# Holding weight loads behind the projections' weights, and splitting the experts' weights, in a Mamba-2 + MLP + mixture-of-experts kernel

## The chip, the cores and the metric

The kernel runs on one core of a Trainium2 chip. Time is device time in microseconds (us), from launch to the end of the program. A core has TensorE (PE in the profile; its weight load is PEld), VectorE (DVE), ScalarE (ACT), GpSimd (POOL) and SyncE (SP). Each works through its own instructions in the order in which the program lists them, and waits at an instruction until the semaphores it needs are there. DMAs are issued by SyncE (most loads), ScalarE (stores) and GpSimd (gathers and scatters by index); 16 DMA engines carry them.

## The reference

Input x has 2048 rows of 512 floats. All is float32.

```
a = layernorm(x)
r = rmsnorm(a, ln1);  z, xb, B, C, dt = split(r @ in_proj)      # 512 -> 2576
xb, B, C = silu(causal conv over 4 rows)
y = chunked state space recurrence (16 heads, chunks of 128 rows) + D * xb
h = a + rmsnorm(y * silu(z), norm_w) @ out_proj                 # 1024 -> 512
m = h + (silu(h2 @ gate) * (h2 @ up)) @ down,  h2 = rmsnorm(h, ln2)   # 512 -> 2048 -> 512
x1 = x + m
n = layernorm(x1);  the two best of 8 experts for each row, weights by softmax
out = x1 + sum over the two of weight * ((silu(n @ Wg[e]) * (n @ Wu[e])) @ Wd[e])   # 512 -> 352 -> 512
```

## The kernel before

The rows are worked in 8 blocks of 256 (two chunks of 128 each) for the recurrence, in 4 blocks of 512 for the MLP, and in tiles of 128 rows sorted by expert for the experts.

**Normalisation and projection.** `load_x` brings x in by 128 rows (t = 0 to 15), into five buffers; the first four are loaded at the start, the fifth (t = 4, the first of block 2; the program calls it x_524) when block 0's recurrence begins in the program. `prepare(b)` takes the statistics of the block's two row tiles (L149, L150), normalises them to `hn` (L219), turns them (L201) into `hT` (L205), and makes from `hT` the time steps `pdt` (L239) and, through a chain of small operations on VectorE and Exp on ScalarE, the decays. These go through DRAM (`rowsd`, L278, L279) and come back spread over the partitions as `cum` and `ec` (`spread`, L312, L324). `first_rows` holds block 1's statistics behind those of block 0; block 2's are not held. The projection of a block takes ten pairs of 128 columns: six (`project`: xb, B, C) and four (`gate`: z). Each pair's weight `wi` (512 KB) is loaded two pairs ahead into three buffers (`load_w_in`, L99), so a load waits until TensorE is done with the pair three before. `project` copies the product out of PSUM on ScalarE (`pre`, L352), VectorE makes the convolution (`ca`, L359, L361), ScalarE the silu (L367). Block 0's six pairs come first, alone; from then on each block's recurrence runs beside the next block's projection.

**Recurrence.** `chunk` takes Exp of `cum` on ScalarE (L420), multiplies on VectorE (L422), the products on TensorE (L414, L437, L445, L452), and the output projection with `w_o` (2048 KB, loaded once, L803; scaled once on POOL, L813; used at L490).

**MLP.** `feed_forward(fb)` works 16 pieces of 128 of the 2048 hidden columns. Its products are made by a scheme that saves multiplications and needs sums of the weights: for fb = 0 `load_early` and `load_late` load the raw parts (`mg`: three loads of 128 KB, `ms`: one of 256 KB) and POOL makes the sums (L531, L532, L542, L543), which ScalarE stores to DRAM; later fb load the stored sums. `mg` and `ms` share three buffers. `load_down` loads the second matrix, 256 KB each piece (`md`, four buffers, L552). fb = 0 begins on TensorE in block 2, at about 222 us.

**Experts.** During the last MLP block `load_expert` loads all eight experts (`ew`, 1408 KB of Wg and Wu and 704 KB of Wd each): a one-column copy on POOL that reads the newest MLP product paces each load.

**What sets the order.** A scheduler orders each engine's instructions (TensorE's from block 2 on is fixed by the program), with its own idea of how long a load takes; `tc.issue_after(i)` makes what is inside wait its turn behind the instruction `i` in the order of issue. SyncE's loads are one queue.

Of the kernel before, what the change touches and what calls it, by code (L numbers as in the profile page):

```python
# [16 lines left out]
P = 128  # L17
T = 2048
D = 512
NK = D // P  # L20
# [14 lines left out]
NE = 8  # L35
EI = 352
# [18 lines left out]
def mamba_mlp_moe(ctx, tc, x, w_in, w_out, w_gu, w_down, par, wr, wg, wu, wd, out):  # L55
# [3 lines left out]
    nc = tc.nc  # L59
# [27 lines left out]
    w_o = pw.tile([P, 8, D], F32, name="w_o")  # L87
# [5 lines left out]
    w_in_k = w_in.rearrange("(k p) n -> p k n", p=P)  # L93
    nc.sync.dma_start(out=w_dt, in_=w_in_k[:, :, 2560:2576])

    def load_w_in(pair):

        w = pw.tile([P, NK, 2 * P], F32, name="wi", tag="wi", bufs=3)
        nc.sync.dma_start(out=w, in_=w_in_k[:, :, pair * 2 * P : (pair + 1) * 2 * P])  # L99
        return w  # L100

    ahead = [load_w_in(pair) for pair in range(2)]
# [9 lines left out]
        out=tri, in_=ones, pattern=[[1, P]], compare_op=ALU.is_ge, fill=0.0, base=0, channel_multiplier=-1  # L112
# [192 lines left out]
    def spread(b, j, rows_d):  # L305

        t = b * NCH + j
        heads = rows_d[:, j * NH : (j + 1) * NH, :]
        cum = []
        for gp in range(2):  # L310
            c = wa.tile([P, 8, P], F32, name=f"cum{t}_{gp}", tag="cum", bufs=3)
            nc.sync.dma_start(out=c, in_=bc(heads[0, 8 * gp : 8 * gp + 8], 0, P))  # L312

            nc.gpsimd.affine_select(  # L314
                out=c, in_=c, pattern=[[0, 8], [1, P]], compare_op=ALU.is_ge, fill=-3.0e38,
                base=0, channel_multiplier=-1,
            )
            cum.append(c)
        ec = None
        if t:  # L320
            ec = wa.tile([P, 2, 4, P], F32, name=f"ec{t}", tag="ec")
            for g in range(4):
                part = slice(g % 2 * HD, (g % 2 + 1) * HD)
                nc.sync.dma_start(out=ec[part, g // 2], in_=bc(heads[1, 4 * g : 4 * g + 4], 0, HD))  # L324
        return cum, ec

    def finish(steps):
        while True:
            try:
                next(steps)  # L330
            except StopIteration as end:
                return end.value
# [187 lines left out]
    KH = NK // 2  # L520
# [3 lines left out]
    def load_early(fb, c):  # L524

        w = pmlp.tile([P, 4, KH, FC], F32, name="mg", tag="mg", bufs=3)
        if fb == 0:
            nc.sync.dma_start(out=w[:, 0], in_=w_gu[c, :, 0, 0])
            nc.sync.dma_start(out=w[:, 1], in_=w_gu[c, :, 1, 1])
            nc.sync.dma_start(out=w[:, 3], in_=w_gu[c, :, 1, 0])  # L530
            nc.gpsimd.tensor_tensor(w[:, 1], w[:, 3], w[:, 1], ALU.add)  # L531
            nc.gpsimd.tensor_tensor(w[:, 2], w[:, 1], w[:, 0], ALU.subtract)  # L532
        else:
            nc.sync.dma_start(out=w[:, 0:3], in_=early_d[c])
        return w
# [14 lines left out]
    def load_down(c):  # L550
        d = pmlp.tile([P, D], F32, name="md", tag="md", bufs=4)
        nc.sync.dma_start(out=d, in_=w_down[c * FC : (c + 1) * FC, :])  # L552
        return d
# [12 lines left out]
    newest = None  # L566
# [127 lines left out]
    def feed_forward(fb):  # L694

        nonlocal mlp_w, newest
        if fb == 0:
            w = load_early(0, 0)
            mlp_w = w, load_late(0, 0, w)
        b11, b21, b22, t1, t2, t3, t4 = sums(fb)  # L700
        rows = []
        pair = None
        made = {}

        def product(ps, w, m, first=True):
            for k in range(KH):
                nc.tensor.matmul(  # L707
                    ps, w[:, k], m[:, k], start=(first and k == 0), stop=(k == KH - 1), skip_group_check=True
                )

        early, late = mlp_w
        for c in range(NFC):
            more = fb < NFB - 1 or c < NFC - 1
            to = (fb, c + 1) if c < NFC - 1 else (fb + 1, 0)
            if more:
                coming = load_early(*to)
            if c == 1:  # L720
                for j in range(NJ):
                    rows.append(wk.tile([P, D], F32, name=f"r{fb}_{j}", tag="row", bufs=5))
                    nc.sync.dma_start(out=rows[j], in_=resd[fb * NJ + j])
            if c > 1 and c % 2 == 0:
                pair = [made.pop(n) for n in (c - 2, c - 1)]
            a = wk.tile([P, 2, FH], F32, name=f"a{fb}_{c}", tag="a", bufs=4)
            up = wk.tile([P, FH], F32, name=f"up{fb}_{c}", tag="up", bufs=2)
            x1 = bank("g", [FH], f"px{fb}_{c}")
            x2 = bank("u", [FH], f"py{fb}_{c}")

            def p2():
                product(x2, late[:, 2], b21)
                with tc.high_priority(AT_ONCE):
                    nc.vector.tensor_tensor(a[:, 0], a[:, 0], x2, ALU.add)
                nc.scalar.activation(a[:, 0], a[:, 0], AF.Silu)

            def p3():
                product(x2, late[:, 1], b22, False)
                with tc.high_priority(AT_ONCE):
                    nc.vector.tensor_tensor(a[:, 1], a[:, 1], x2, ALU.add)  # L740
                nc.scalar.activation(a[:, 1], a[:, 1], AF.Silu)

            def p5():
                product(x2, early[:, 1], t1)
                with tc.high_priority(AT_ONCE):
                    nc.scalar.copy(up, x2)


            order = [p2, p5, p3] if c == 0 else [p5, p3, p2]
            product(x1, early[:, 0], b11)  # L750
            with tc.high_priority(AT_ONCE):
                nc.scalar.copy(a[:, 0], x1)  # L752
            order[0]()
            if pair:
                mlp_down(fb, rows, 2 * (c % 2), pair)
            yield
            product(x1, early[:, 2], t2, False)
            with tc.high_priority(AT_ONCE):
                nc.scalar.copy(a[:, 1], x1)
            order[1]()  # L760
            if more:
                coming = coming, load_late(*to, coming)
            yield
            product(x1, late[:, 0], t3, False)
            with tc.high_priority(AT_ONCE):
                nc.vector.tensor_tensor(up, up, x1, ALU.add)  # L766
            order[2]()
            yield
            product(x1, late[:, 3], t4, False)
            with tc.high_priority(AT_ONCE):  # L770
                nc.vector.tensor_tensor(a[:, 0], a[:, 0], x1, ALU.mult)
            nc.gpsimd.tensor_tensor(a[:, 1], a[:, 1], up, ALU.mult)  # L772
            if pair:
                mlp_down(fb, rows, 2 * (c % 2) + 1, pair)
            newest = a.rearrange("p h q -> p (h q)")
            made[c] = newest, load_down(c)
            if more:
                early, late = coming
            yield
        if more:  # L780
            mlp_w = coming
        pair = [made.pop(n) for n in (NFC - 2, NFC - 1)]
        for j in range(NJ):
            mlp_down(fb, rows, j, pair)
        yield
        yield from route(fb, rows)
# [9 lines left out]
    for pair in range(6):  # L796
        finish(project(0, pair, hT, *xc))
        if pair < 2:
            next(coming)
        elif pair == 2:  # L800
            ready = finish(coming)
            near = [spread(0, 0, ready[-1])]
    nc.sync.dma_start(out=w_o, in_=w_out.rearrange("(t p) n -> p t n", p=P))  # L803
    near.append(spread(0, 1, ready[-1]))
    xbts[0] = turned_x(0, xc[0])

# [109 lines left out]

    def load_expert(e, part):

        gu = ew[:, e, :NG].rearrange("p (k a n) -> p k a n", k=NK, a=2)
        d = ew[:, e, NG:].rearrange("p (m n) -> p m n", m=len(ET))  # L920
        for lo in (part * EI,) if part < 2 else (NG, NG + 2 * D):
            nc.gpsimd.tensor_copy(ew[: EI - 2 * P, e, lo : lo + 1], newest[: EI - 2 * P, 0:1])
        if part < 2:
            nc.sync.dma_start(out=gu[:, :, part, :], in_=(wg, wu)[part][e].rearrange("(k p) n -> p k n", p=P))
        else:
            nc.sync.dma_start(out=d[:, 0:2, :], in_=wd[e, 0 : 2 * P, :].rearrange("(k p) n -> p k n", p=P))
            nc.sync.dma_start(out=d[: EI - 2 * P, 2, :], in_=wd[e, 2 * P : EI, :])


# [75 lines left out]
        first = yield from table(NS1, "1")  # L1005

    tail = routed(tail)
    parts = [(e, part) for e in range(NE) for part in range(3)]
    for n in range(4 * NFC):
        next(feed)  # L1010
        if n % 4 == 2:
            next(tail, None)

        if n % 5 in (0, 2) and parts:
            load_expert(*parts.pop(0))
    assert first and not parts

# [176 lines left out]
```

## Time and profile before

| | us |
|---|---|
| median of 3 runs (lowest to highest) | 1541.81 (1540.99 to 1544.17) |
| the profiled execution's own time | 1540.27 |
| its span, first to last instruction | 1538.6 |
| TensorE matmul busy | 1498.3 |
| VectorE, ScalarE, GpSimd busy | 749.8, 744.0, 425.5 |

The span is shorter than the execution by what lies around the program. A row of the timeline is start, duration, engine, line, operation, tiles (written<-read), shape and count, and in brackets how long the engine had been idle and what ended that. A wait is put down to what came last. The granted clock of TensorE was 0.994 in the mean.

### The profile page before, as it was taken

How to read it: one execution, taken by the hardware profiler on the slowest of the kernel's cores; microseconds unless marked ns; L12 is line 12 of the kernel's file. 1: busy time of each engine (PE TensorE's matmuls, PEld its weight loads, DVE VectorE, ACT ScalarE, POOL GpSimd, SP SyncE). 2: the span in 40 equal slices, each digit the busy share in tenths (PEclk: the TensorE clock that was granted, in tenths of full speed). 3: DMA queues.
4: the chain of work that ended last, by engine and by line, in shares of the span. 5: the costliest groups of instructions: out<-in, count | busy, mean ns of one | idle time of the engine just before them, and what ended most of it. 6: DMA issues, size and time to landing. Idle time of an engine off the chain costs nothing. (4 is left out here: it accounts for less than half of the span.)

```text
span 1538.6 us, 18825 instructions
## 1 busy us (share of the span) xinstructions
PE 1498.3 (97%) x6153; PEld 1021.0 (66%) x6153; DVE 749.8 (49%) x1939; ACT 744.0 (48%) x1332; POOL 425.5 (28%) x537
## 2 busy tenths in 40 slices
PE   8899999999999999999999999999999999999996
PEld 7566577677667676767676677666776666566553
DVE  7776775645645564556454643334343433222221
ACT  5888967635663598458745754222221231111110
POOL 4432324424242212141212120411131124233321
PEclk9999999999999999999999999999999999999999
DMA  9444445545544554454335532426879434333332
GB/s 305 137 138 125 137 140 183 190 149 171 171 151 148 185 165 131 137 118 157 121 123 179 167 121 89 93 93 209 289 205 260 152 91 64 66 69 65 66 63 35
DMA packets 128241, 217.54 MB, mean 141 GB/s; under 512 B 12560, under 2 KB 72848, under 8 KB 128144
## 3 DMA queue, kind: packets, MB, share of 16 engines
q1 hardware_dynamic: 105376, 166.34, 35.6%
q0 software_dynamic: 9088, 18.91, 7.2%
q10 hardware_dynamic: 13680, 31.07, 5.4%
q8 instruction: 52, 0.85, 0.2%
q14 instruction: 45, 0.37, 0.1%
HBM read 175.48 MB, written 40.80 MB: 141 GB/s over the span
## 5 line engine op out<-in xcount | busy, mean ns | idle before, releaser
L691 PE MATMUL pd<-md,a 128*128 128x512 f32 x512 | 238.8, 593 | 0.8 <-DVE r L692 0.7
L340 PE MATMUL pm<-hT,wi 128*128 128x256 f32 x768 | 185.4, 386 | 3.7 <-DMA wi<-in_w_in 3.7
L340 PEld LDWEIGHTS pm<-hT,wi 128*128 128x128 f32 x768 | 141.7, 192 | 29.2 <-issue 7.9
L692 DVE TENSOR_TENSOR r<-r,pd 128x512 f32<-128x512 f32 x128 | 87.4, 684 | 150.6 <-PE pd L691 149.9
L691 PEld LDWEIGHTS pd<-md,a 128*128 128x128 f32 x512 | 96.9, 190 | 76.6 <-issue 65.8
L361 DVE SCALAR_TENSOR_TENSOR ca<-pre,params,ca 128x256 f32<-128x256 f32 x288 | 143.9, 557 | 0.3
L707 PE MATMUL py<-h2T,ms 128*128 128x256 f32 x512 | 131.7, 380 | 3.5 <-DMA ms<-late 2.6
L772 POOL TENSOR_TENSOR a<-a,up 128x256 f32<-128x256 f32 x64 | 47.0, 734 | 265.7 <-DVE up L766 225.8
L340 PE MATMUL pz<-hT,wi 128*128 128x256 f32 x512 | 117.0, 381 | 0.0
L490 PE MATMUL po<-w_o,zs 128*128 128x512 f32 x256 | 116.2, 607 | 0.0
L1045 PE MATMUL epg<-ew,xgT 128*128 x288 | 109.0, 460 | 0.2 <-ACT xgT L203 0.2
L1045 PE MATMUL epu<-ew,xgT 128*128 x288 | 108.7, 459 | 0.0
L707 PEld LDWEIGHTS py<-h2T,ms 128*128 128x128 f32 x512 | 95.4, 190 | 19.5 <-issue 2.3
L420 ACT ACT_TABLE_LOAD x75 | 96.2, 1283 | 21.5 <-DVE ncum L285 14.5
L340 PEld LDWEIGHTS pz<-hT,wi 128*128 128x128 f32 x512 | 94.8, 190 | 13.8 <-ACT zs L373 0.8
L1066 PE MATMUL epd<-ew,ehT 128*128 (+1 forms) x216 | 98.9, 593 | 1.0 <-DVE ehT L1059 1.0
L420 ACT ACTIVATE cum<-cum,ncum 128x128 f32<-128x128 f32 x256 | 85.7, 392 | 6.2 <-POOL cum L314 4.8
L490 PEld LDWEIGHTS po<-w_o,zs 128*128 128x128 f32 x256 | 49.5, 195 | 58.4 <-issue 57.3
L752 ACT COPY a<-px 128x256 f32<-128x256 f32 x64 | 23.6, 369 | 127.2 <-PE px L707 111.3
L1026 POOL DMA_INDIRECT xg<-xnd,idx x36 | 35.5, 985 | 154.4 <-PE pt L201 150.6
L422 DVE SCALAR_TENSOR_TENSOR cum<-cum,dt,psc 128x128 f32<-128x128 f32 x256 | 72.9, 339 | 5.8 <-PE psc L414 3.6
L203 ACT COPY xgT<-pt 128x512 f32<-128x512 f32 x36 | 21.0, 586 | 111.8 <-PE pt L201 111.8
(240 smaller groups left out, 2528.1 us busy)
## 6 DMA issues: line engine op xcount, KB each, us to landing
wi<-in_w_in SPq DMA_DIRECT2D x80, 512.0 KB, 3.8
ms<-late SPq DMA_DIRECT2D x48, 512.0 KB, 3.7
mg<-early SPq DMA_DIRECT2D x48, 384.0 KB, 3.8
md<-in_w_down SPq DMA_DIRECT2D x64, 256.0 KB, 4.0
cum<-rowsd SPq DMA_DIRECT2D x32, 512.0 KB, 4.1
late<-ms ACTq DMA_DIRECT2D x16, 512.0 KB, 2.7
ec<-rowsd SPq DMA_DIRECT2D x60, 128.0 KB, 3.4
xnd<-xn ACTq DMA_DIRECT2D x28, 256.0 KB, 3.8
```

The source lines that it names most:

```text
L340: nc.tensor.matmul(pm[:, m, :], w[:, k, m * P : (m + 1) * P], hT[:, k, :], start=(k == 0), stop=(k == NK - 1))
L361: nc.vector.scalar_tensor_tensor(ca, pre[:, m, k : k + TB], cw[:, k : k + 1], ca, ALU.mult, ALU.add)
L420: nc.scalar.activation(lt[:, half, i], lt[:, half, i], AF.Exp, bias=ncum[:, j, h : h + 1])
L422: nc.vector.scalar_tensor_tensor(lt[:, half, i], lt[:, half, i], dt[:, j, h : h + 1], psc[:, half, i], ALU.mult, ALU.mult)
L490: nc.tensor.matmul(po, y[:, m, :], w_o[:, m, :], start=(m == 0), stop=(m == 7))
L691: nc.tensor.matmul(pd, a[:, j * P : (j + 1) * P], d, start=(m == 0), stop=(m == 1))
L692: nc.vector.tensor_tensor(rows[j], rows[j], pd, ALU.add)
L707: nc.tensor.matmul(ps, w[:, k], m[:, k], start=(first and k == 0), stop=(k == KH - 1), skip_group_check=True)
L772: nc.gpsimd.tensor_tensor(a[:, 1], a[:, 1], up, ALU.mult)
L1026: nc.gpsimd.indirect_dma_start(out=xg, out_offset=None, in_=src, in_offset=bass.IndirectOffsetOnAxis(ap=idx[:, n : n + 1], axis=0))
L1045: nc.tensor.matmul(ps, xT[:, k, :], w[:, lo : lo + EI], start=(k == 0), stop=(k == NK - 1))
L1066: nc.tensor.matmul(pd, hT[:n, m, :], w[:n, NG + m * D : NG + (m + 1) * D], start=(m == 0), stop=(m == len(ET) - 1))
```

## The change

It does three things. `loaded` keeps the newest in-projection weight load; w_o's load, the first MLP's first weights and the first MLP's down weights are placed behind it in the order of issue (w_o behind the load that is newest at the end of block 0's projections, and the first MLP's weights behind the one that is newest when that MLP begins). The first `spread` stands after the fifth projection pair in place of the third. The experts' weights are loaded in 48 pieces (Wg and Wu in halves of 352 KB, Wd in 512 and 192 KB), one on three of four steps of the last MLP block, in place of 24 calls with 32 loads on two of five.

```diff
+    loaded = None
     def load_w_in(pair):
+        nonlocal loaded
         w = pw.tile([P, NK, 2 * P], F32, name="wi", tag="wi", bufs=3)
-        nc.sync.dma_start(out=w, in_=w_in_k[:, :, pair * 2 * P : (pair + 1) * 2 * P])
+        loaded = nc.sync.dma_start(out=w, in_=w_in_k[:, :, pair * 2 * P : (pair + 1) * 2 * P]).ins
...
         if fb == 0:
-            w = load_early(0, 0)
+            with tc.issue_after(loaded):
+                w = load_early(0, 0)
             mlp_w = w, load_late(0, 0, w)
...
-            made[c] = newest, load_down(c)
+            with ExitStack() if fb else tc.issue_after(loaded):
+                made[c] = newest, load_down(c)
...
         elif pair == 2:
             ready = finish(coming)
+        if pair == 4:
             near = [spread(0, 0, ready[-1])]
-    nc.sync.dma_start(out=w_o, in_=w_out.rearrange("(t p) n -> p t n", p=P))
+    with tc.issue_after(loaded):
+        loaded = nc.sync.dma_start(out=w_o, in_=w_out.rearrange("(t p) n -> p t n", p=P)).ins
...
     def load_expert(e, part):
...
-        for lo in (part * EI,) if part < 2 else (NG, NG + 2 * D):
-            nc.gpsimd.tensor_copy(ew[: EI - 2 * P, e, lo : lo + 1], newest[: EI - 2 * P, 0:1])
-        if part < 2:
-            nc.sync.dma_start(out=gu[:, :, part, :], in_=(wg, wu)[part][e].rearrange("(k p) n -> p k n", p=P))
-        else:
-            nc.sync.dma_start(out=d[:, 0:2, :], in_=wd[e, 0 : 2 * P, :].rearrange("(k p) n -> p k n", p=P))
+        half, a = divmod(part, 2)
+        ks = slice(half * KH, (half + 1) * KH)
+        lo = (half * NK + a) * EI if part < 4 else NG + 2 * a * D
+        nc.gpsimd.tensor_copy(ew[: EI - 2 * P, e, lo : lo + 1], newest[: EI - 2 * P, 0:1])
+        if part < 4:
+            nc.sync.dma_start(out=gu[:, ks, a, :], in_=(wg, wu)[a][e].rearrange("(k p) n -> p k n", p=P)[:, ks])
+        elif a == 0:
+            nc.sync.dma_start(out=d[:, 0:2, :], in_=wd[e, 0 : 2 * P, :].rearrange("(k p) n -> p k n", p=P))
+        else:
             nc.sync.dma_start(out=d[: EI - 2 * P, 2, :], in_=wd[e, 2 * P : EI, :])
...
-    parts = [(e, part) for e in range(NE) for part in range(3)]
+    parts = [(e, part) for e in range(NE) for part in range(6)]
...
-        if n % 5 in (0, 2) and parts:
+        if n % 4 != 1 and parts:
```

The scheduler lays the engines' orders anew. SyncE's first loads in both programs (lines of before):

```
before: x x x x params w_dt wi wi wr wi w_o x_524 mg mg wi mg ms mg wi rowsd mg mg md cum
        rowsd cum wi wi cum wi ec*4 wi md md wi md wi cum ...
after:  x x x x params w_dt wi wi wr wi x_524 wi wi rowsd wi rowsd cum wi cum cum wi w_o
        ec*4 wi wi wi cum ...   (mg mg mg ms mg mg mg wi md ms only behind the 32nd wi)
```

VectorE's first instructions, with the statistics of x_524 marked:

```
before: ... stats(x_83) stats(x_85) ... hT hT ... hn v hn u dt ... dA stats(x_524) rows ... ncum ca
after:  ... stats(x_83) stats(x_85) ... stats(x_524) hT hT ... hn v hn u dt ... dA rows ... ncum ca
```

## The prediction

> **What bounds the kernel now.** I read the engine shares first, then who waited for whom, then the first 75 us in order of time, since the page shows that nothing later has room.
>
> ```profile
> PE 1498.3 (97%) x6153; PEld 1021.0 (66%) x6153; DVE 749.8 (49%) x1939; ACT 744.0 (48%) x1332; POOL 425.5 (28%) x537
> ...
> PE pc L273 <- DVE dA L270: 5.3, 3, 2.9
> PE pm L340 <- DMA wi<-in_w_in: 3.7, 1, 3.7
> ...
> PE py L707 <- DMA ms<-late: 2.6, 2, 1.9
> ```
>
> TensorE sets the time: 1498.3 of 1538.6 us. About 40 us are idle, and the change can only save what of these is a DMA's: 3.7 us once for an in-projection weight, and 2.6 us twice in all for an MLP weight. Where the 3.7 us lie, and what comes with them, the timeline (start, duration, engine, line) and the table by stretch (length; busy time of each engine; granted clock, DMA share, GB/s) tell:
>
> ```profile
> 8.31 1.27 DVE L205 TENSOR_TENSOR hT<-pt,params 128x512 f32<-128x512 f32 x2
> ...
> 19.48 0.70 DVE L149 BATCH_NORM_STATS2 bn<-x 128x6 f32<-128x512 f32 x1 [0.37 <-DMA x<-in_x]
> ...
> 9.04 1.96 PE L239 MATMUL pdt<-w_dt,hT 128*128 128x16 f32 x16 [0.75 <-DVE hT L205]
> ...
> 34.08 5.38 PE L340 MATMUL pm<-hT,wi 128*128 128x256 f32 x16 [3.71 <-DMA wi<-in_w_in]
> ...
> 22.89 0.59 ACT L352 COPY pre<-pm 128x512 f32<-128x512 f32 x1 [0.42 <-PE pm L340]
> ...
> 39.55 0.59 ACT L352 COPY pre<-pm 128x512 f32<-128x512 f32 x1 [3.44 <-PE pm L340]
> ...
> 34.10:37.70 3.60, 3.60 (x9) 2.86 (x10) 2.88 (x7) 2.00 (x3) 1.30 (x3) 0.53 1.07 353
> 37.70:39.60 1.90, 1.90 (x12) 1.65 (x11) 1.66 (x4) 0.05 (x1) 0.20 (x1) 1.00 0.52 110
> 39.60:67.50 27.90, 26.27 (x131) 18.96 (x129) 19.63 (x56) 27.51 (x43) 11.12 (x10) 1.00 0.47 142
> ```
>
> Three things. The sixth projection waits 3.71 us for its weight and then runs 3.6 us at half clock: 5.38 us where the same 16 matmuls later take 3.62 (196.84), so the stall costs 3.71 + 1.76 = 5.5 us on TensorE. ScalarE idles with it (3.44 us), and from 39.6 to 67.5 it is the full engine, 27.51 of 27.90 us: what reaches ScalarE late ends late. And VectorE takes the statistics of the fifth x row block (x_524) only at 19.48, long after hT at 8.31.
>
> **The change, part by part.**
>
> *Order of the loads.* Without w_o (2048 KB) and the first MLP weights, SyncE issues the third in-projection load, then x_524, then only loads that wait for TensorE. The sixth load, issued 27.21 and landed 6.7 us later (33.9), is then issued when the third projection ends and has 7 us until its use, with only one small load and 512 KB at a time around it (lone ones land in 3.7 us). The stall at 34.08 goes.
>
> *What else the order moves.* In the program order of the changed kernel the statistics of x_524 stand on VectorE **before** the two hT (rows 18, then 19 and 20); before, some 30 places behind them. VectorE runs in order, so hT now waits for x_524, and behind hT everything else on VectorE, pdt on TensorE, and the Exp chain of ScalarE. When does that land? Its issue moves from 8.69 to about 6.6, right behind the third weight load. The views of single tiles give the landings:
>
> ```profile
> L99 SPq DMA_DIRECT2D wi<-in_w_in x1: 1321/1321/1321, 5.3 to 5.3; - x1
> ...
> DMA to landing us min/median/max: 8.2/8.2/8.2
> ...
> L83 SPq DMA_DIRECT2D x<-in_x x1: 1608/1608/1608, 8.7 to 8.7; - x1
> ...
> DMA to landing us min/median/max: 10.8/10.8/10.8
> ```
>
> The third weight load was issued at 5.27 and landed at 13.5; x_524, issued 8.69 behind w_o (6.63 + 12.1 = 18.7), landed at 19.5, 0.7 us after it. The first two weight loads landed at 8.7 and 10.5: every one of SyncE's loads landed in the order of issue. So x_524 lands 0.6 to 0.7 us behind the third weight: 14.1. Here a rule speaks the other way: the Trainium skill, DMA: Bandwidth & Descriptors, section Queues, rings and completion order, says that completion is not in issue order per issuing engine, a later small transfer can complete first. By the rule x_524 could land with the median of the x loads, 6.6 + 4.1 = 10.7, and the sum below would be 3.4 us less. I take the landings of this trace.
>
> *The sum of the head.* Statistics 14.1 to 14.8, first hT done 15.45, so pdt starts at 15.5 instead of 9.04: +6.5. TensorE has then been idle for 7 us and starts at half clock; the two places in this trace with such a start (34.08, and 71.9 after 2.9 us idle) lost 1.8 us each: +1.8. The projections follow without a break, so ScalarE's third copy (22.89) comes 8.3 later, at 31.2. From there ScalarE's own work is the chain: until 39.6 it had gaps of 0.88, 0.20 and 3.44 us, which close because VectorE has its inputs and the sixth projection no longer waits: -4.5. VectorE also gains: the POOL operations on the first MLP weights (22.0 to 28.0) go, beside which the convolution's steps took up to 0.97 us for 0.48. That lets VectorE keep up; it is not counted again. Head: 6.5 + 1.8 - 4.5 = **+3.8**, between +2 and +5.5 (1 us either way on the landing, the slow start only half paid). The later gaps up to 220 us wait on ScalarE and VectorE, not on the clock, and move along.
>
> *Spread two pairs later.* ScalarE's, VectorE's and TensorE's order up to 80 us is that of before except for two transposes; the first cum load moves from 25.84 to about 31 and lands (3.5 us) at 34.6, its first Exp is due at about 40. Nothing, with 5 us of cover.
>
> *First MLP weights at 220 us.* They were loaded in the first 50 us; now four loads follow the weight load issued at 217.03, when the third gate ends. Issues every 0.45 us; alone the weight lands at 220.8, then 128 KB every 0.35 us (231.68 and 232.07 landed 0.33 apart): the three parts of mg by 221.8, ms by 222.5. TensorE wants mg at 222.07, ms at 222.94: covered by 0.3 and 0.4. POOL's three sums (0.73, 0.72, 0.72 at 253.78 to 255.71) end at about 224.1 where TensorE wants the last at 223.80: **+0.3**, from 0 to +4 (a late ms and another half-clock start). POOL is free then: its next work is at 230.79. On SyncE the second group stands before the next weight load (222.27) and adds 1.4 us of issue in a queue that waits for TensorE there anyway; the second ms still waits for TensorE at 225.6, and behind it stand the third mg, the decay rows and a weight load as before. The down weights, one behind each weight load, have 25 us or more. ScalarE's stores of these weights (first at 198.28) move along, 0.33 us each, on an engine that is half idle there. w_o, issued at about 39 and landed by 47, is first used by POOL at 58: nothing. The loads issued behind it (ec, and two weight loads) are wanted after 58.
>
> *Experts in 48 pieces.* 16 more copies on POOL at 0.14 to 0.18 us (28% busy), 16 more issues at 0.4 us on SyncE: hidden. The skill's page has a rule against it (sections Anatomy of one DMA and Bandwidth: about 2 us fixed per transfer, so batch to 1 MiB or more), by which 16 more would be an estimated 32 us of transfers. The trace has 192 KB landing in 6.5 us where 704 KB land in 6.5 to 7.0, overlapped with the rest, and nobody on TensorE waits for them: 0. The two waits for ms (at 1155 and 1167) lie beside the scatter of the lists, when every load took 10 us. Counted in program order, the bytes ahead of these two ms loads go from 1600 and 1792 KB to 1792 and 1600. **0**, from -2.6 to +2.6.
>
> Sum: +4.1 us on the profiled execution's 1540.27 is 1544.4. That execution is 1.54 below the median of the runs, 1541.81; I add the same difference: **1545.9 us**, 0.27% slower. A measurement tells about 0.2%, 3.1 us, from no change.
>
> **The rivals.**
> - *x_524 lands early* (faster). If the rings share between transfers, it lands at 9.4 (the shortest x load, 2.8 us) or sooner; hT is then at most 1.8 us late, TensorE idle for 2.5 us and still at its clock, and the head gains 4.5 - 1.8 = 2.7, up to 4.5; with the 0.3 at 220 us 1537.6 to 1539.4. It decides at a landing of 10.3: later than that the half-clock start is paid and nothing is left. For it: the rule above. Against it: strict order in every landing of the first 20 us. 0.13.
> - *VectorE's relief is worth more than I say, or the order of blocks 1 and 2, which the scheduler laid anew, closes a gap* (the pc wait at 70 us is 2.9 us; TensorE's idle time from 100 to 250 us makes 6): half the loss comes back, +1 to +3, 1543 to 1545: no difference. 0.27.
> - *The first MLP weights come late* (slower still). If the loads share with the weight load before them, ms comes 2 us late, TensorE waits and starts at half clock, +3.8 more: 1549.7. For it: covers of 0.3 us. Against it: loads of that size landed within 3 us elsewhere. 0.15.
> - The main case, +2.5 to +6: 0.45.
>
> **The numbers.** The main case and the late weights are slower, but a small part of the main case stays within 0.2%: slower 0.58, same 0.29, faster 0.13. The range leaves out the best end of the first rival and a pile-up of both losses: 1538.8 to 1550.5.
>
> **What would show it.** After: a VectorE wait for x before hT of about 6 us; pdt starting near 15.5 at half clock; no wait of pm for wi; ScalarE without its 3.4 us gap; the third gate followed by px with a wait under 0.5 us. If hT still starts near 8.3, or if ScalarE reaches the end of its full stretch before 67.5, the prediction is wrong.

## The result: 15 us slower, and the profile after

| us | before | after |
|---|---|---|
| median (4 runs each; lowest to highest) | 1542.18 (1540.99 to 1544.17) | 1557.71 (1555.02 to 1559.48) |
| profiled execution, its span | 1540.27, 1538.6 | 1556.15, 1554.4 |
| its granted clock, mean | 0.994 | 0.989 |

The ratio after to before is 1.0098, 95% interval 1.0077 to 1.0119: about 15 us slower, where 4 were forecast and 8.7 was the edge of the range. First the engine shares and who waited for whom on TensorE (total, times, longest):

```profile
PE 1504.5 (97%) x6153; PEld 1026.6 (66%) x6153; DVE 741.5 (48%) x1939; ACT 744.7 (48%) x1333; POOL 427.1 (27%) x553
...
PE pdt L242 <- DVE hT L208: 7.4, 1, 7.4
PE pt L204 <- ACT zs L376: 3.7, 1, 3.7
PE px L711 <- ACT a L756: 3.3, 3, 1.7
...
PE po L493 <- POOL w_o L820: 3.1, 1, 3.1
...
PE py L711 <- DVE a L738: 1.9, 1, 1.9
...
PE pc L276 <- DVE dA L273: 0.8, 2, 0.4
```

The wait of pm for wi is gone, as forecast, and five waits are new or have grown (all but pc's). Only the first, pdt for hT, was in the forecast. Setting each TensorE instruction of one trace against the same one of the other gives how far after lies behind, by the time in before: +11.2 us at 27, +6.5 at 60, +2.3 at 75, +7.2 at 91, +3.7 at 160, +6.3 at 200, +9.5 at 222, +15.75 at 243, and +15.6 at the end. So after 243 us nothing is lost on balance. (Near 850 us px waits 2.63 us for VectorE's `a` in both traces; it is no part of the change. In after, half clock follows this wait and costs 1.5 us; in before none does, but it waits 2.6 us for `ms` near 1160, where after waits 0.4.)

**The head.** VectorE, then TensorE, in after:

```profile
14.67 0.69 DVE L152 BATCH_NORM_STATS2 bn<-x 128x6 f32<-128x512 f32 x1 [6.32 <-DMA x<-in_x]
15.28 1.27 DVE L208 TENSOR_TENSOR hT<-pt,params 128x512 f32<-128x512 f32 x2
...
16.00 3.60 PE L242 MATMUL pdt<-w_dt,hT 128*128 128x16 f32 x16 [7.36 <-DVE hT L208]
```

The statistics of x_524 hold hT as forecast. What TensorE's clock does then, by stretch (length; busy time of each engine; granted clock, DMA share, GB/s):

```profile
16.00:20.00 4.00, 4.00 (x17) 3.91 (x18) 1.56 (x7) 0.00 (x0) 0.00 (x0) 0.50 0.00 0
20.00:24.40 4.40, 4.40 (x12) 3.50 (x11) 2.35 (x12) 0.33 (x2) 0.00 (x0) 0.50 0.00 0
24.40:30.00 5.60, 5.60 (x26) 4.58 (x24) 3.55 (x15) 1.36 (x3) 0.27 (x2) 0.98 0.32 94
```

Half clock for at least 8.4 us of work, where the forecast took 3.6: half of that, 4.2 us, is lost, hence +11.2 = 7.0 for the late hT and 4.2 for the clock. ScalarE's third copy comes at 34.06 (+11.2), its zs of the third gate at 65.84 where before had 59.37 (+6.5): the closed gaps gave 4.7, as forecast.

**Block 0's output projection.** TensorE in before, then in after:

```profile
70.34 0.38 PE L273 MATMUL pc<-tri,dA 128*32 128x128 f32 x2 [2.88 <-DVE dA L270]
```

```profile
74.30 0.38 PE L276 MATMUL pc<-tri,dA 128*32 128x128 f32 x2 [0.38 <-DVE dA L273]
84.38 1.13 PE L493 MATMUL po<-w_o,zs 128*128 128x512 f32 x2 [3.06 <-POOL w_o L820]
```

Before waited 2.88 us for dA at this pc and none for w_o. After it is the other way round: what the one wait gives back the next one takes, and 3.4 us of half clock follow in both (at 71.7 in before, at 86.1 in after).

**Block 3's hT.** VectorE's rows and TensorE's pt in after, then the two VectorE rows of before that answer to them:

```profile
205.86 2.14 DVE L425 SCALAR_TENSOR_TENSOR cum<-cum,dt,psc 128x128 f32<-128x128 f32 x8
207.93 1.21 DVE L431 TENSOR_TENSOR xd<-xbt,dtdec 128x1024 f32<-128x1024 f32 x1
...
209.72 1.96 DVE L222 TENSOR_SCALAR hn<-x,mv,rboth 128x512 f32<-128x512 f32 x2
...
210.41 1.08 PE L204 MATMUL pt<-ident,hn 128*128 128x128 f32 x4 [3.65 <-ACT zs L376]
```

```profile
195.82 1.97 DVE L219 TENSOR_SCALAR hn<-x,mv,rboth 128x512 f32<-128x512 f32 x2
...
203.14 1.22 DVE L428 TENSOR_TENSOR xd<-xbt,dtdec 128x1024 f32<-128x1024 f32 x1
```

In before hn stands ahead of xd, in after behind it. TensorE's pt (it turns hn) at 210.41 needs the first of the two hn, done at 210.26; it has waited 3.65 us and runs at half clock. The clock is half from 209.0 to 215.8 in after; before has such a stretch there too, from 208.2 to 211.6. The profile puts this wait down to ScalarE's zs, done at 210.33; that hn is the cause is for an experiment to show.

**The first MLP.** VectorE's small steps `acc` (a polynomial for the time steps of block 3) with TensorE's py behind them, and POOL's sums of the weights, in after; the same steps in before; and POOL, ScalarE and TensorE in after at the second piece:

```profile
232.54 3.74 DVE L264 SCALAR_TENSOR_TENSOR acc<-acc,s 128x32 f32<-128x32 f32 x7
...
236.43 0.41 DVE L738 TENSOR_TENSOR a<-a,py 128x256 f32<-128x256 f32 x1
...
236.90 1.13 PE L711 MATMUL py<-ts,mg 128*128 128x256 f32 x4 [1.88 <-DVE a L738]
...
233.11 0.72 POOL L535 TENSOR_TENSOR mg<-mg 128x256 f32<-128x256 f32 x1
233.91 0.78 POOL L546 TENSOR_TENSOR ms<-ms,mg 128x256 f32<-128x256 f32 x1
```

```profile
222.48 1.55 DVE L261 SCALAR_TENSOR_TENSOR acc<-acc,s 128x32 f32<-128x32 f32 x7
```

```profile
249.32 0.72 POOL L535 TENSOR_TENSOR mg<-mg 128x256 f32<-128x256 f32 x1
...
250.08 0.33 ACTq L547 DMA_DIRECT2D early<-mg  x1
250.45 0.37 ACT L756 COPY a<-px 128x256 f32<-128x256 f32 x1 [3.35 <-POOL pre L356]
...
250.96 1.10 PE L711 MATMUL px<-ts,mg 128*128 128x256 f32 x4 [1.67 <-ACT a L756]
```

With POOL adding beside it, VectorE takes 3.74 us for seven steps that took 1.55; behind them stands the sum `a` for which py waits 1.88. And ScalarE stands 3.35 us at a store of POOL's sums (the last is done at 250.04, the store goes out at 250.08), ahead of the copy for which px waits 1.67.

### The profile page after: what moved, and what is told of

Same layout as the page of the kernel before. It is cut to its first block, busy times and chain, and to the rows that moved or that the text cites. A ratio compares the mean times of both kernels' runs of the same rounds, so it can differ in the third digit from the quotient of the medians.

```text
span 1554.4 us, 18886 instructions
## 1 busy us (share of the span) xinstructions
PE 1504.5 (97%) x6153; PEld 1026.6 (66%) x6153; DVE 741.5 (48%) x1939; ACT 744.7 (48%) x1333; POOL 427.1 (27%) x553
## 5 line engine op out<-in xcount | busy, mean ns | idle before, releaser
L364 DVE SCALAR_TENSOR_TENSOR ca<-pre,params,ca 128x256 f32<-128x256 f32 x288 | 136.0, 529 | 0.3
L1056 PEld LDWEIGHTS epu<-ew,xgT 128*128 128x128 f32 x288 | 54.7, 190 | 30.5
```

Of the source, the lines that this page charges most:

```text
L364: nc.vector.scalar_tensor_tensor(ca, pre[:, m, k : k + TB], cw[:, k : k + 1], ca, ALU.mult, ALU.add)
L1056: nc.tensor.matmul(ps, xT[:, k, :], w[:, lo : lo + EI], start=(k == 0), stop=(k == NK - 1))
```

## The experiments

They ran in five sets on three chips: 0 (e0, e1, e2, e4, e5, e6, e10, e11), 13 (e8 and e12 to e18) and 6 (e19, e20). The runs of the kernel before lie between 1538 and 1555 us there, so each time is given as a ratio to the runs of before in its own set, with a 95% interval. e0 is before on chip 0, e12 after on chip 13; traces are compared with these two, also across the chips, and only by the matched TensorE instructions.

**e0, before again; e12, after again** (no edit).

> The kernel before, unchanged, profiled on the chip of this series so that traces are compared on one chip. Both theories: as its own runs beside it, 1545 to 1553; no wait of pt for zs at 205, wait of pm for wi near 34, waits of pc for dA near 70 and 150.

> The changed kernel, unchanged, timed and profiled on the chip of this series, so that its trace stands beside those of the experiments. Every theory: 1.008 to 1.012 of before; the wait of hT for x near 6 us, po for w_o, pt for zs at 210 and the four waits of the first MLP's start as in its first profile.

e0: 0.9988 (0.9969 to 1.0007). e12: 1.0063 (1.0043 to 1.0082), under the expected 1.008 and a little less than after's first ratio, the intervals just overlapping. By the same matching e12 is behind e0 by 9.5 us at 30, 5.0 at 58, 6.2 at 145, 5.1 at 201, 9.7 at 230, 14.7 at 244, 11.6 at the end: the same three places. In e12 TensorE waits for dA (3.17) and not for w_o; in e0 for both (2.33 and 0.76). The sum of the two is 2.9, 3.1, 3.4 and 3.2 in before, e0, after and e12: what the first takes, the second does not. An expectation failed there too: the wait for w_o is not in every execution.

**e6, only w_o held; e4, only the first MLP's weights held; e5, only the pieces; e8, only the later spread.** Each is before with one part of the change's diff.

> The kernel before, with only w_o held behind the projections' weights. Its order has the statistics of x_524 ahead of hT, as the changed kernel's has. Theory A: VectorE waits 6 us for x_524, pdt starts near 16 at half clock, and po waits for w_o near 84: 1548 to 1551. Rival B (the head alone is given back by the gap of 2.9 us at 70): 1541 to 1545.

> The kernel before, with only the first MLP's first weights and its down weights held behind the projections' weights (w_o, spread and the experts' loads as before). Theory A: POOL's six sums fall at 222 to 228 us beside VectorE's small operations there, which stretch, and ScalarE's stores wait for POOL; TensorE loses 4 to 6 us between 222 and 245: 1546 to 1549, less up to 3 if the queue without these loads shortens the wait for wi at 34. Rival B (the loss there in the changed kernel comes of the state in which block 2 reached it): 1540 to 1543.

> The kernel before, with only the experts' weights in 48 pieces. Theory A: nothing before 850 us moves; the two waits for ms (2.6 us together) shrink by 0 to 2.4 and little else changes: 0 to 2.4 us under the kernel before. Rival B (each further transfer costs its 2 us of fixed time on the queue, and a wait appears behind it): slower than before by 2 us or more.

> The kernel before, with only the first spread moved two pairs later. Every theory: nothing waits for it; within 1.5 us of before, 0.999 to 1.001. If it is over 3 us slower, the later spread is a part of the loss that the prediction put at nothing.

| | ratio to before | interval |
|---|---|---|
| e6, w_o held | 1.0088 | 1.0065 to 1.0111 |
| e4, MLP weights held | 1.0018 | 1.0008 to 1.0028 |
| e5, 48 pieces | 0.9992 | 0.9983 to 1.0002 |
| e8, spread later | 0.9975 | 0.9965 to 0.9986 |

Holding w_o alone loses as much as the whole change, 14 us, more than the 6 to 9 that theory A gave it (B, with next to nothing, falls): it has hT late, and its trace also has the pt wait of 3.7 and ScalarE's px waits (3.2 in 4). Holding the MLP's weights loses 3; its trace is 7 us ahead of e0 at 44 us, because the wait for wi at 34 is gone, and 3 behind at 244, after the pt wait (3.65) and the first MLP. The pieces alone do nothing that these runs can tell, and rival B falls; its 2 us are the figure that the prediction takes from the Trainium skill. The later spread, which every theory had at nothing, gains 4 us. What TensorE did there in e8 and in e0, and SyncE's loads of both (start, issue time):

```profile
25.83 7.93 PE L343 MATMUL pm<-hT,wi 128*128 128x256 f32 x36
```

```profile
35.71 6.64 PE L340 MATMUL pm<-hT,wi 128*128 128x256 f32 x16 [3.58 <-DMA wi<-in_w_in]
```

```profile
24.07 0.38 SPq L102 DMA_DIRECT2D wi<-in_w_in  x1
...
25.76 0.33 SPq L315 DMA_DIRECT2D cum<-rowsd  x1
26.88 0.38 SPq L102 DMA_DIRECT2D wi<-in_w_in  x1
```

```profile
26.32 0.33 SPq L312 DMA_DIRECT2D cum<-rowsd  x1
...
27.18 0.41 SPq L312 DMA_DIRECT2D cum<-rowsd  x1
27.68 1.19 SPq L99 DMA_DIRECT2D wi<-in_w_in  x2
```

The sixth weight load is the one issued at 24.07 in e8 and the first of the two at 27.68 in e0, where it stands behind two cum loads of 512 KB that have to wait for the decay rows. So the stall at 34 was in good part the spread's own doing, and moving the spread alone takes it away. Holding the MLP's weights alone does so too, with the spread early (e4, which issues the sixth load at 23.38): either is enough.

**e1, the statistics of x_524 behind dA.** After, with

```diff
...
-        with tc.issue_after(first_rows) if b == 1 else ExitStack():
+        with tc.issue_after({1: first_rows, 2: first_dA}[b]) if b in (1, 2) else ExitStack():
             scales(b)
...
+        made_dA = nc.vector.tensor_tensor(dA, dt, bc(a_neg, 1, NCH), ALU.mult)
+        if b == 0:
+            first_dA = made_dA.ins
...
```

> The changed kernel, with one thing put back: the statistics of x_524 (and with them block 2's scales) are held behind block 0's dA on VectorE, so that hT does not stand behind them. Theory A (about 7 of the 15.5 us lost come from the head: hT 7 us late, 4.2 us of half clock after it, and POOL's scaling of w_o that carries this past TensorE's next gap): hT back at 8.3, pdt at 9.0, no half clock at 16, no wait of pm for wi at 34, no wait of po for w_o; 1546 to 1551 us. Rival B (the scheduler's new orders in blocks 1 and 2 lose it, and the head is only where it starts): the head is back and the time is still above 1554.

1.0011 (0.9999 to 1.0023). pdt starts at 8.99 for 1.96 us; no half clock at 16 (3.4 us of it from 11.9 on, as in e0 from 11.0); no wait for wi. Against after (1.0063 to 1.0098) 8 to 13 us are back, about the 7 to 12 that A gave: B falls. po still waits 1.5 for w_o, where A had no wait. Its trace leads e0 by 8 us at 201 and trails it by 5 at 244: the pt wait of 3.66 and the MLP's waits are unchanged.

**e2, TensorE kept busy through the wait.** After, with `idling(56)` for `idling(5)`.

> The changed kernel, with 56 in place of 5 idle transposes on TensorE behind block 0's second turn, so that TensorE works through the wait for hT (8 to 16 us). Theory A: the wait for hT stays 6.3 us on VectorE, but pdt takes 2.0 us in place of 3.6 and the projections run at full clock; the 4.2 us of half clock between 16 and 25 us are gone, and 3 to 4.2 of them arrive at the end: 1553.5 to 1555. Rival B (ScalarE or VectorE bounds the head, the clock costs nothing): 1557 to 1558.

1.0080 (1.0049 to 1.0112): no gain over after that these five runs can tell. pdt took 1.96 and the projections ran at full clock: TensorE was 5.2 us behind e0 at 28.5 where e12 was 9.5, so the half clock does cost TensorE 4.3. But at 57 e2 was 3.9 behind and e12 5.0, with VectorE and ScalarE late (py waits 3.2 for cum). The 51 transposes also gave ScalarE another order, with its silu and copies the other way round, and the profiled execution, the fastest of the five, is 5.1 us ahead of e12 at 244. So what the clock costs at the end of the program is not settled.

**e10, block 3's hn ahead.** After, with `tc.high_priority(AT_ONCE)` around scales and hn for b == 3.

> The changed kernel, with block 3's statistics and normalisation (hn) raised in priority, so that VectorE does them before the chunk's cum products and xd, as the kernel before does. Theory A (the wait of 3.65 us that the profile puts down to zs at 210, and the half clock after it, come from hn standing behind xd on VectorE): that wait is gone, 3 to 5 us faster than the changed kernel, 1.0065 to 1.008 of before. Rival B (ScalarE's zs itself is late, held by its cs chain): the wait stays, 1.009 to 1.010 of before.

1.0049 (1.0031 to 1.0066). No wait of pt for zs at 210. TensorE, then ScalarE:

```profile
206.91 0.60 PE L204 MATMUL pt<-ident,hn 128*128 128x128 f32 x4
...
210.07 0.58 ACT L376 ACTIVATE zs<-pz 128x512 f32<-128x512 f32 x1
```

pt now runs 3 us ahead of the zs that the profile of after names, so it does not need that zs. From 201 to 215 us its trace gains about 2 on e0 where e12 loses about 2. As after's two ratios are 1.0063 and 1.0098, the time gains some 2 to 8 us (the 2, against e12, are within the intervals). A holds: the wait that the profile puts down to zs was hn's (e13's profile names hn itself, 5.0 us at the same pt).

**e13, the MLP's weights six loads earlier.** After, with `issue_after(newest_loads[-6])` for the first MLP's first weights.

> The changed kernel, with the first MLP's first weights held six projection weights earlier (the down weights as in the changed kernel), so that POOL makes its sums some 40 us before TensorE wants them. Theory A (4 to 6 us are lost at the first MLP because POOL's sums run beside VectorE's small steps, which take 0.53 us there for 0.22, and because ScalarE's stores wait for the sums): py, pc and px no longer wait at 237 to 251, or by half as much, and the kernel is 3 to 6 us faster than the changed kernel. Rival B (the waits come of VectorE and ScalarE being behind by then whatever the loads do): within 2 us of the changed kernel.

1.0051 (1.0034 to 1.0069), as e12 within the intervals. POOL's sums are out of the way, and six of VectorE's steps take 1.32 us again; the py wait is gone. But between 230 and 244 us it still loses 5.3: ScalarE stands 4.32 us at the store ahead of the copy for px. So B by the time, A for the one wait: a second cause stands right behind the first.

**e18, the stores of the sums on POOL.** After, with

```diff
-            nc.scalar.dma_start(out=early_d[c], in_=w[:, 0:3])
-            nc.scalar.dma_start(out=late_d[c], in_=v)
+            nc.gpsimd.dma_start(out=early_d[c], in_=w[:, 0:3])
+            nc.gpsimd.dma_start(out=late_d[c], in_=v)
```

> The changed kernel, with the stores of the first MLP's weight sums issued by POOL in place of ScalarE, nothing else. Theory A: of the 5 us lost between 229 and 243 us the px waits for a (1.7 us, and those after 300) go, the py wait (POOL's sums beside VectorE) and the pc wait for xbt stay: 2 to 3 us faster than the changed kernel. Rival B: as the changed kernel, 1.006 to 1.009 of before.

1.0043 (1.0031 to 1.0055): 3 to 8 us faster than after's two ratios (the 3, against e12, are within the intervals). The px waits are gone; ScalarE's copy now waits only for its product:

```profile
252.25 0.37 ACT L756 COPY a<-px 128x256 f32<-128x256 f32 x1 [0.28 <-PE px L711]
...
234.68 3.01 DVE L264 SCALAR_TENSOR_TENSOR acc<-acc,s 128x32 f32<-128x32 f32 x7
```

VectorE's steps beside POOL are still slow (0.43 us each), and py's wait grew to 2.80. In its trace the gain on e12 is only 1.6 us by 260; 2.0 more come up to 800, and 1.7 at 865, where e12 alone has half clock.

**e11, w_o held with the head and hn mended, MLP weights early, spread early; e15, four mends on after** (e1, e10, e13, and w_o scaled early as in e14).

> w_o held behind the projections' weights and 48 pieces as in the changed kernel; the statistics of x_524 behind block 0's dA, block 3's hn raised in priority, the first MLP's weights loaded early and the first spread after the third pair as in the kernel before. Theory A (the losses are the head, hn of block 3 and POOL's sums beside VectorE at the first MLP, and all three are taken away here): the stall for wi at 34 is gone, and 1 to 4 us faster than before. Rival B (the orders laid anew lose elsewhere): 2 us or more slower than before.

> The changed kernel with the four mends together: the statistics of x_524 behind dA, block 3's hn raised in priority, w_o scaled ahead of block 0's last cum, the first MLP's first weights held six weights earlier. Theory A (these four are where the 15 us went): nothing is left of them, and the wi wait of before at 34 is gone too: 0.996 to 0.9995 of before. Rival B (the scheduler loses elsewhere what is mended here): 1.002 or more.

e11: 1.0017 (1.0002 to 1.0033). e15: 0.9977 (0.9963 to 0.9991). e11 missed, and shows why the early loads are no way out: the store that waits for POOL now stands in the head, ahead of the Exp of block 0's time steps (ScalarE):

```profile
17.52 0.33 ACTq L549 DMA_DIRECT2D early<-mg  x1
17.88 1.28 ACT L254 ACT_TABLE_LOAD   x1 [5.44 <-DMA mg<-in_w_gu]
...
19.18 0.23 ACT L254 ACTIVATE u<-u 128x32 f32<-128x32 f32 x1
```

pc waits 3.26 us at 25 for it, and from 229 to 244 another 3.6 go. e15 met A's range. It is 7 us ahead of e0 until 201 us and loses 5.2 from 229 to 244, at ScalarE's stores.

**e14, w_o scaled early.** Before, with POOL's scaling ahead of block 0's last cum:

```diff
...
+    weigh(8)
     near.append(spread(0, 1, ready[-1]))
...
```

> The kernel before, with POOL's eight scalings of w_o placed ahead of the last cum of block 0, in the time (43 to 56 us) in which POOL waits for that load. Theory A (TensorE's waits of pc for dA at 70 and of po for w_o at 80 are one chain: together 2.9 to 3.5 us in every profile of before and after, however split): po no longer waits for w_o, and the half clock behind such a wait goes when both are short: 0 to 3 us faster than before. Rival B (VectorE, slowed by POOL beside it, makes everything later): 1 to 3 us slower.

0.9962 (0.9942 to 0.9982): 6 us faster than before, more than expected. POOL and TensorE:

```profile
43.53 12.95 POOL L810 TENSOR_SCALAR w_o<-w_o,params 128x512 f32<-128x512 f32 x8
...
72.08 0.38 PE L273 MATMUL pc<-tri,dA 128*32 128x128 f32 x2 [1.53 <-DVE dA L270]
```

POOL does it while it would wait for cum, as in before:

```profile
56.76 1.09 POOL L314 TENSOR_SCALAR_AFFINE_SELECT cum<-cum 128x1024 f32<-128x1024 f32 x1 [14.22 <-DMA cum<-rowsd]
```

The pc wait is 1.53 and po has none: the chain behind the second of them was POOL's. B, a slower VectorE, falls.

**e16, the four mends and the stores on POOL; e20, three mends alone** (e1, e10, e18); **e17, before with e14 and the pieces; e19, before with e8, e14, the pieces and the stores on POOL.**

> All four mends (as e15), and the stores of the first MLP's weight sums issued by POOL, which makes the sums, in place of ScalarE. Theory A (ScalarE stands at a store, waiting for POOL, ahead of the copies that TensorE wants): the wait of px for a at 240 goes, 2 to 4 us faster than e15: 0.994 to 0.997 of before. Rival B (POOL's own issue of a store takes as long and delays its sums): within 1 us of e15 or slower.

> The changed kernel with three mends alone: the statistics of x_524 behind dA, block 3's hn raised in priority, the stores of the weight sums issued by POOL. Theory A (these three made the loss, and what stays of the change gains at 34 us): 0.995 to 0.999 of before; waits left are py for a at 230 (POOL's sums beside VectorE, 2 to 3 us) and po for w_o. Rival B (a part of the loss is elsewhere): over 1.002.

> The kernel before, with w_o scaled ahead of block 0's last cum (e14) and the experts' weights in 48 pieces (e5), nothing held. Theory A (the two are far apart in time and add up): 4 to 8 us faster than before, 0.995 to 0.9975. Rival B (the pieces' gain was chance): as e14 within 1 us.

> The kernel before, with the first spread two pairs later (e8), w_o scaled early (e14), 48 pieces (e5) and the stores of the weight sums issued by POOL; no load is held. Theory A (the gains are at different places: 34 us, 80 us, 1160 us): 8 to 12 us faster than before, 0.992 to 0.995. Rival B (the spread's gain and the early scaling's are the same slack of ScalarE's chain in the head): 4 to 6 us, 0.996 to 0.9975.

| | ratio to before | interval |
|---|---|---|
| e16 | 0.9930 | 0.9906 to 0.9953 |
| e20 | 0.9961 | 0.9950 to 0.9973 |
| e19 | 0.9968 | 0.9958 to 0.9978 |
| e17 | 0.9973 | 0.9963 to 0.9983 |

e20 is the answer: with three mends and every load held as in the change, the kernel is 6 us *faster* than before. Against e12 it is 9.6 us ahead at 27 us, 9.7 at 205, 13.9 at 230, 16.0 at 255 and 18.4 at 1500: the head and block 3's hn make up most of it, the first MLP 2. Two waits are left, the first of them at the MLP, the other at block 0's output projection:

```profile
PE py L713 <- DVE a L740: 3.2, 1, 3.2
...
PE po L495 <- POOL w_o L822: 0.9, 1, 0.9
```

e16 takes both of these away as well, and is the fastest run: 11 us under before, more than its expectation for A. What the traces lose against e0 between 224 and 250 us sets the two causes at the first MLP apart:

| POOL's sums | stores on ScalarE | stores on POOL |
|---|---|---|
| as in after | 7.8 (e12) | 6.2 (e18), 5.6 (e20) |
| made earlier | 6.1 (e13), 5.2 (e15) | 0.7 (e16) |

Either mend alone leaves most of the loss; e16 differs from e15 in the stores alone, and it goes. The kernel before with the stores alone on POOL was not run, so how much of e20's and e16's lead over before is a gain that before could have too is open. e17 met the small end of its range; the gain over e14 is within the intervals, so that the pieces add is not shown. e19 missed A and fell in B's range; B's reason is not shown by it, since its order again has hn of block 3 behind xd, and the pt wait of 3.7.

## Why the prediction was wrong, by its own steps

- *The stall for wi goes*: right, in after and in every kernel that held w_o or the MLP's weights. Its cause was read too narrowly: the queue ahead of the sixth load also held cum loads, and e8, which moves only the spread, removes it too. So the step *spread later: 0* was wrong by about 4 us of gain (when done alone).
- *x_524's statistics ahead of hT*: right. Forecast: statistics 14.1, pdt 15.5; measured 14.67 and 16.00. So x_524 landed just before 14.67, close to what the order of issue gives (14.1) and not at the 10.7 of the other reading. The rule of the Trainium skill weighed there (DMA: Bandwidth & Descriptors, Queues, rings and completion order) says that completion need not follow the order of issue; it does not speak of size, its example is a later transfer on one DMA engine behind one on sixteen. By it the rival *x_524 lands early* was made. It did not happen here.
- *Half-clock start +1.8*: mis-sized on TensorE, 4.2 (4.3 by e2). I took it from starts after 2.9 and 3.7 us of idle and called them the two in the trace; before has two more (at 150 and 208 us, after 2.0 and 1.6 us of idle). All four had 3.4 us of half clock. This start came after 7.4. One trace was too little for the size: the stall at 34 itself was followed by 6.0 us of half clock in e0. Whether those 2.4 us reach the end, e2 did not settle.
- *ScalarE's gaps -4.5*: right, 4.7. So the head stood at +6.5 at 60 us, where +3.8 was forecast.
- *The later gaps up to 220 us move along*: **this step failed first.** I had compared the orders up to 80 us, found them nearly the same, and took the rest as rigid. They are not: the scheduler had put block 3's hn behind xd on VectorE, and from it come the pt wait of 3.65 and half clock (e10). From 200 to 222 us +3.2. The rival *a closed gap gives half back* failed on the other side: the pc gap closed, and the wait for w_o took it, because both hang in part on POOL's chain (with w_o scaled early, e14, the one shrinks to 1.53 and the other goes).
- *First MLP +0.3*: **this step failed second**, and by most: +6.2 from 222 to 243. The sum itself was right, px waited 0.31 for POOL's mg, and no load was late. But it asked only when POOL's sums are ready for TensorE, not what they do to VectorE beside them, though the prediction had the number (0.97 for 0.48 near 26 us) and used it as a gain for the head alone; and it put ScalarE's stores at 0.33 us each on "an engine that is half idle", where one that waits for POOL holds the copies behind it. The two causes stand in parallel: e13 removes the first and e18 the second, and each leaves over 6 of e12's 7.8 us; e16 removes both, and 0.7 is left. The rival *the first MLP weights come late* had the place and the sign, and a wrong mechanism.
- *48 pieces: 0*: right (e5). The skill's figure for small transfers, by which the prediction reckoned an estimated 32 us, is given there for transfers that GpSimd issues; these are SyncE's, and nothing of it shows.
- *What would show it*: every sign that the prediction named came true (VectorE's wait for x of 6.32, pdt at 16.00 at half clock, no wait for wi, no gap of 3.4 us on ScalarE, px behind the third gate waiting 0.31 at most). They test the head's order and the arrival of the loads, which were right; none asks about hn in block 3 or about what POOL's sums hold up.

The sum of after, on the profiled executions: head 6.5 (forecast 3.8), blocks 1 to 3 a further 3.0 (0), first MLP 6.2 (0.3), the rest -0.1 (0): 15.6 against 4.1.

## What to carry to other kernels

A held load does not only move a load: where a scheduler lays the orders, each engine's whole order has to be compared, to the end of the stretch in which the held data is first used, and above all for the in-order engines whose next instruction TensorE wants. When work is moved into a busy place, ask three things of each instruction: who is slowed beside it, what stands behind it on its queue (a store that waits for another engine holds every copy after it), and which second wait is just shorter than the one removed. When removing one cause changes nothing, look for a second one in parallel before giving up on the first: e13 and e18 each take under 2 of the 7.8 us, both together (e16) take 7.1.

## What the runs showed of the hardware

- VectorE's scalar-tensor-tensor steps of 128x32 took 0.22 us each alone (before, 222.48) and 0.53 beside POOL's sums of 128x256 (after, 232.54); 0.22 again where POOL was elsewhere (e13, 236.00).
- TensorE's granted clock was full or half in these traces, and half in stretches of 3.41 us or a multiple of it (before: four of 3.4 us in the first 250; after: 13.7 us from 11.0 on, of which 5.0 fell in the idle time and 8.6 in work). How long TensorE had been idle does not by itself tell when: 1.55 us of idle near 206 in before (with 0.67 just ahead of it) were followed by half clock, while one and the same wait of 2.63 us was followed by full clock in before and by half in e0 (before, then e0; the same four matmuls take 1.13 and 1.93 us):

```profile
848.47 1.13 PE L707 MATMUL px<-h2T,mg 128*128 128x256 f32 x4 [2.63 <-DVE a L771]
```

```profile
853.86 1.93 PE L707 MATMUL px<-h2T,mg 128*128 128x256 f32 x4 [2.63 <-DVE a L771]
```

- The long start of after began with 16 matmuls of 16 columns, behind 7.4 us of idle; which of the two made it long was not tried.
- The same program's executions on one chip differ by up to 1% (before on chip 13: 1538.7 to 1555.4), and the time goes with the mean granted clock: among the 59 runs of before beside e8, the eight at 0.990 took 1547.3 us in the mean, the nine at 0.994 took 1541.7. A single profile can hold waits of 2 to 3 us that another profile of the same kernel lacks (3.06 for w_o in after, none in e12); one trace against one trace is no measure below that.
